# A graph layer's score table and its input rows read by SyncE and ScalarE in place of GpSimd, the first tile in five parts

## The chip, the cores and the metric

The kernel runs on one core of one Trainium2 chip. The metric is device time in microseconds for one execution. A core has TensorE (PE), VectorE (DVE), ScalarE (ACT), GpSimd (POOL) and SyncE (SP); SP, ACT and POOL can start DMAs, each on a queue of its own, and all run in the order of their own instruction streams, tied together by semaphores. PEld is TensorE's load of weights, which overlaps its matmuls.

## The reference

Two layers of a graph network on 625 nodes of 1,024 features and 10,000 edges. Each layer adds a graph part, a linear attention and a feed-forward part to x. The change lies in the first layer. Cut to what matters:

```
xn = layernorm(x)
# graph attention, 4 heads of 64
xl, xr = (down(xn) @ Wl), (down(xn) @ Wr)
e      = sum(leaky_relu(xl[src] + xr[dst]) * att)    # one score per edge and head
alpha  = softmax of e over the edges of each dst     # self loops added
gat    = segment_sum(alpha * xl[src], dst) @ W_up
# linear attention
mix    = attention(xn) @ W_o + b_o
x      = x + gat + mix
x      = x + ffn(layernorm(x))                       # quantised, 256 wide inside
...                                                  # then the second layer
```

## The kernel before, in words

Rows of x are worked in five tiles of 125 nodes (NT = 5, P = 125), tile t being nodes 125t to 125t + 124.

**Scores.** While TensorE does the linear attention's products, POOL gathers rows of xl and xr for 128 edges at a time by indirect DMA (L621), DVE and ACT make exp(score) of them, and POOL scatters these (L641) into `table`, a dense array in DRAM with four values (the heads) for each pair of source and destination. There are 79 scatters; each writes the same array, so each waits for the one before. An earlier DMA has set the table to zero, and `CT` in SBUF holds how many edges each pair has.

**Sums (weigh, sums, turn_sums, up_again).** When all scatters have landed, `load_table(t)` reads the table's tile t: 125 sources on partitions, five source groups s, 125 destinations and four heads, some 1.25 MB. `rows_dma` (L180) makes two DMAs of each read, rows 0 to 111 and rows 112 to 124. `weigh(t)` multiplies it on DVE by CT, one instruction for each s (L865), into `pT`. `sums(t)` has TensorE add up over the five s, 20 products of 65 columns (`pg`, L137; each appears as two records); DVE divides (L898 to L902); `turn_sums(t)` transposes on TensorE (L912) and copies by ACT (L916); `up_again(t)` multiplies by W_up (`px`, L928) and DVE adds that into x (L933). For tiles other than 3, `px` in PSUM already holds the attention's product with W_o.

**x and the bias.** x is read again from DRAM (`x`, 125 rows by 1,024, two DMAs a tile), since the first copy's room is used up. b_o is added by `add_bias(t)` on DVE in two additions of 512 columns (L1072); for tile 3 the kept product with the bias is added instead.

**Order.** The order on every engine is written by hand. POOL reads table tile 0, x(0), table tile 1, x(1) to x(4). DVE does weigh(0). Then a loop over p runs sums(p), turn_sums(p), weigh(p + 1), load_table(p + 2), the biases and up_again(p), with the feed-forward steps of tile p - 1 between them. add_bias(0, 1) comes in round 0 behind weigh(1), add_bias(3) in round 1 behind weigh(2), add_bias(2, 4) at the start of round 2. Round 1 also gives SP the loads of the second layer's first weights, `lin1.weights(0)` (L124: two DMAs of 1,024 KB for L1_Wk, two for L1_Wv), behind load_table(3) in the text. Round 0 makes POOL clear a margin of xnT1 and load `bq`.

The table tiles and `pT` share a pool of four buffers (`mid`), so a table tile can be read only when the buffer's last reader is done: tile 2 waits for the first sums, tile 3 for the second, tile 4 for the third.

Of the kernel before, what the change touches and what calls it, by code (L numbers as in the profile page):

```python
# [14 lines left out]
ALU = mybir.AluOpType  # L15
# [5 lines left out]
NT = 5  # L21
P = 125
# [31 lines left out]
def attempt(ctx: ExitStack, tc: tile.TileContext, w: dict, out: bass.AP, shifted: bool):  # L54

    nc = tc.nc
# [101 lines left out]
    def nodes(t):  # L158
        return slice(t * P, (t + 1) * P)
# [18 lines left out]
    def rows_dma(eng, dst, src):  # L178

        return [eng.dma_start(out=dst[lo:hi], in_=src[lo:hi]) for lo, hi in ((0, 112), (112, P))]  # L180
# [6 lines left out]
    xrows = w["x"].rearrange("(t p) d -> t p d", p=P)  # L187
# [35 lines left out]
    hold = {}  # L223

    def mid(shape, name):
        return midp.tile(shape, FP, tag="mid", name=name)

    def bigT(name):
        return big.tile([128, KC, NP], FP, tag="big", name=name, padded_shape=[128, KC, 640])
# [133 lines left out]
    with ExitStack() as st0:  # L363
# [5 lines left out]
        tview = table[0:N * N, :].rearrange("(u p d) h -> p u (d h)", u=NT, p=P)  # L369
        xnT = bigT("xnT")  # L370

        with ExitStack() as edges:
# [385 lines left out]
            def mixed(t, ks=range(KC), keep=None, then=None, paced=True, cs=(0, 1)):  # L758
                for c in cs:
                    def pe(c=c):  # L760
                        if c == 0 and ks[0] == 0:
                            hold["px", t] = ps2("px1")
                        for k in ks:
                            made = nc.tensor.matmul(hold["px", t][:P, c, :], lhsT=oT[:, k, nodes(t)], rhs=wo[c](k),  # L764
                                                    start=(k == 0), stop=(k == KC - 1 and keep is not None))
                        latest["pe"] = made.ins.name

                    def after():
                        px = hold.pop(("px", t))
                        for c in range(2):  # L770
                            nc.vector.tensor_tensor(keep[:, c, :], px[:P, c, :], bo[c][:P], op=ALU.add)

                    do(None, pe, after if keep is not None and c == 1 else None)
                    if then is not None and c == 0:
                        then()
                    if paced:
                        work(0.87 * len(ks))
# [49 lines left out]
            bo = [lin.bias(w["L0_bo"], c, tag) for c, tag in enumerate(("bk_t", "bv_t"))]  # L827
# [4 lines left out]
            kept = mid([P, 2, 512], "kept")  # L832
# [14 lines left out]
        x = xpool.tile([P, NT, D], FP, name="x")  # L847
# [3 lines left out]
        def load_table(t):  # L851

            hold["tb", t] = mid([P, NT, P, 4], "tb")
            if not shifted:
                rows_dma(nc.gpsimd, hold["tb", t].rearrange("p s d h -> p s (d h)"),
                         tview[:, :, t * 4 * P:(t + 1) * 4 * P])

        def weigh(t):

            tb, pT = hold.pop(("tb", t)), mid([P, NT, 4, P], "pT")  # L860
            hold["pT", t] = pT
            if shifted:
                exps(t, tb)
            for s in range(NT):
                nc.vector.tensor_tensor(pT[:, s], tb[:, s].rearrange("p d h -> p h d"),  # L865
                                        CT[:, s, nodes(t)].unsqueeze(1).to_broadcast([P, 4, P]), op=ALU.mult)

        def exps(t, tb):

            for h in range(4):  # L870
                sc = mix.tile([P, NP], FP, tag="qe", name="sc", bufs=1)[:, 0:N].unsqueeze(2)
                nc.sync.dma_start(out=sc, in_=table[0:N * N, :].rearrange("(t p s) h -> t p s h", t=NT, p=P)
                                  [t][:, :, h:h + 1])
                mx = late.tile([P, 1], FP, tag="mx", name="mx", bufs=1)
                nc.vector.tensor_reduce(mx, sc, AX.XY, ALU.max)
                nc.vector.tensor_scalar(mx, mx, -1.0, None, op0=ALU.mult)
                nc.scalar.activation(sc, sc, AF.Exp, bias=mx, scale=1.0)
                for s in range(NT):
                    def pe():
                        pp = ps1("pexT")  # L880
                        nc.tensor.transpose(pp[:P, :P], sc[:, nodes(s), 0], ident[:P, :P])
                        nc.vector.tensor_copy(tb[:, s, :, h], pp[:P, :P])

                    do(None, pe)
# [3 lines left out]
        def sums(t):  # L888
            pT = hold.pop(("pT", t))

            def pe():
                pg4 = hold["pg"] = ps1("pg")[:, :260].rearrange("p (h e) -> p h e", h=4)
                for h in range(4):
                    group(pg4[:P, h, :], [(pT[:, s, h, :], xl1[:, s, h, :]) for s in range(NT)])

            def after():
                pg4 = hold["pg"]
                nc.vector.tensor_scalar(dens[:, t, :], pg4[:P, :, 64], 1e-16 if shifted else 1e-30, None, op0=ALU.add)  # L898
                den = late.tile([P, 4], FP, tag="den", name="den", bufs=2)
                nc.vector.reciprocal(den, dens[:, t, :])  # L900
                go = hold["go"] = late.tile([P, 4, 64], FP, tag="go", name="go", bufs=1)
                nc.vector.tensor_tensor(go, pg4[:P, :, 0:64],  # L902
                                        den.unsqueeze(2).to_broadcast([P, 4, 64]), op=ALU.mult)

            do(None, pe, after)
# [145 lines left out]
            return p1, f1, f2, f3, f4, p5, f5  # L1051


        load_table(0)
        for t in range(NT):
            rows_dma(nc.gpsimd, x[:, t, :], xrows[t])
            if t == 0:
                load_table(1)
        weigh(0)
        kv_pieces = iter([(f, t) for t in range(NT) for f in ("key", "value")])  # L1060
        made_of = {}

        def spacer():

            f, t = next(kv_pieces)
            getattr(lin1, f)(t)

        def add_bias(*ts):
            for t in ts:
                for c in range(2):  # L1070
                    xc = x[:, t, c * 512:(c + 1) * 512]
                    nc.vector.tensor_tensor(xc, xc, kept[:, c, :] if t == 3 else bo[c][:P], op=ALU.add)  # L1072

        degree = mix.tile([128, NP], mybir.dt.int16, tag="degree", name="degree", bufs=1)

        def in_degrees():
            def pe():
                pdeg = hold["pdeg"] = ps2("pdeg")
                for h in range(2):
                    group(pdeg[:, h, :HN], [(ones[:P, :], CT[:, s, h * HN:(h + 1) * HN]) for s in range(NT)])  # L1080

            do(None, pe, lambda: nc.scalar.activation(halves(degree), hold["pdeg"][:, :, :HN], AF.Copy))

        for p in range(NT + 2):
            do()
            if p >= 2 and p != NT:
                made_of[p - 2][5]()
            if 1 <= p <= NT:
                made_of[p - 1] = ffn(p - 1)
                made_of[p - 1][0]()  # L1090
            if p == 1:
                mixed(4, cs=(0,))
            if p == 2:
                add_bias(2, 4)
                in_degrees()
            if p >= 3:
                spacer()
            if p >= 2 and p != NT:
                made_of[p - 2][6]()
            if p == 0:  # L1100
                xnT1 = bigT("xnT1")
                nc.gpsimd.memset(xnT1[:, :, N:NP], 0.0)
                lin1 = LinearAttention(xnT1, ("L1_Wq", "L1_Wk", "L1_bk", "L1_Wv", "L1_bv"), w["L1_bq"],
                                       lambda us: None, nc.gpsimd)
                lin1.large = True
            if p < NT:
                sums(p)
            if 1 <= p <= NT:
                made_of[p - 1][1]()
                do()  # L1110
                if p == NT:
                    made_of[p - 2][5]()
                made_of[p - 1][2]()
                if p == NT:
                    made_of[p - 2][6]()
            do()
            if p < NT:
                turn_sums(p)
            if p + 1 < NT:
                weigh(p + 1)  # L1120
            if p + 2 < NT:
                load_table(p + 2)
            if p < 2:
                add_bias(*((0, 1), (3,))[p])
            if p == 1:
                mixed(4, cs=(1,))
                lin1.weights(0)
                lin1.half(0, loaded=True)
            if 2 <= p <= NT:
                spacer()  # L1130
            if 1 <= p <= NT:
                made_of[p - 1][3]()
            do()
            if p < NT:
                up_again(p)
            if 1 <= p <= NT:
                made_of[p - 1][4]()
# [616 lines left out]
    for i in range(3):  # L1754
        d = 1 << i
# [240 lines left out]
```

## Time and profile before

| what | us |
|---|---|
| median of 3 runs (lowest, highest) | 2182.63 (2180.21, 2184.75) |
| the profiled execution, device time | 2200.8 |
| its span, first to last instruction | 2199.0 |
| PE busy | 2106.0 (96%) |
| DVE busy | 713.1 (32%) |
| POOL busy | 340.3 (15%) |
| ACT busy | 194.7 (9%) |
| mean granted TensorE clock | 0.984 |

How to read it: times within the kernel are microseconds from the first instruction. A timeline line has the start, the duration, the engine, the line of the source, the operation, output<-input, and how many were merged; in brackets stand the engine's idle time before it and what ended that. SPq is SP's instruction that starts a DMA. A line of the list of waits names who waited for whom, the total, how many times, and the longest. In the page's row of slices each digit is the busy share of one fortieth of the span in tenths; PEclk is TensorE's granted clock in the same way. In the stretch from 408 to 410 us the clock is 1.00, from 412 on 0.50, from 456 on 1.00. DMAs move 231 GB/s from 430 to 435 us and 340 GB/s from 465 to 470 us.

### The profile page before, as it was taken

Reading aid. Unit: us, or ns where it says so; the run is one execution under the profiler, and the core shown is the slowest. Engines: PE = TensorE matmul, PEld = TensorE weight load, DVE = VectorE, ACT = ScalarE, POOL = GpSimd, SP = SyncE. Lnnn points to the kernel's source line nnn. Section 1 sums busy time; section 2 is a strip of 40 time slices with the busy share of each in tenths; the row PEclk is TensorE's granted clock in tenths of the full one; section 3 lists DMA queues with packets and bytes.
Section 4 is the critical chain, followed back from the end, with each engine's and each line's share of the span. In section 5 each row is a group of like instructions: output and inputs, shape, how many; then the busy total and the mean of one; then the engine's idle time right before and its main releaser. Section 6 shows DMA issues by size and latency. Waiting matters only on the chain. (4 is left out here: it accounts for less than half of the span.)

```text
span 2199.0 us, 17371 instructions
## 1 busy us (share of the span) xinstructions
PE 2106.0 (96%) x6934; PEld 1205.2 (55%) x6934; DVE 713.1 (32%) x1214; ACT 194.7 (9%) x355; POOL 340.3 (15%) x349
## 2 busy tenths in 40 slices
PE   7989999489899999999999999999999999999998
PEld 6656575155445777754446777457744444444443
DVE  5776478367532740000122143222111111111012
ACT  2000110012211100000000111100000000000000
POOL 1666756500000200210000000110000000000011
PEclk9999999789999999999999999999999999999999
DMA  7623253261122110150203101022099988997742
GB/s 216 205 77 106 81 182 123 58 174 33 39 86 77 48 39 26 62 182 0 101 14 106 59 18 39 29 95 96 28 365 343 330 291 308 331 329 283 277 140 91
DMA packets 145848, 301.62 MB, mean 137 GB/s; under 512 B 12370, under 2 KB 22436, under 8 KB 145754
## 3 DMA queue, kind: packets, MB, share of 16 engines
q1 hardware_dynamic: 123700, 244.23, 31.3%
q0 software_dynamic: 17376, 46.42, 7.3%
q10 hardware_dynamic: 4678, 9.72, 1.4%
q8 instruction: 58, 0.95, 0.2%
q14 instruction: 36, 0.29, 0.0%
HBM read 277.49 MB, written 22.84 MB: 137 GB/s over the span
## 5 line engine op out<-in xcount | busy, mean ns | idle before, releaser
L137 PE MATMUL pu<-w,xgT 128*128 128x512 f32 x768 | 333.9, 593 | 1.9 <-DVE xgT L1290 1.9
L137 PEld LDWEIGHTS pu<-w,xgT 128*128 128x128 f32 x768 | 144.0, 190 | 174.8 <-issue 172.0
L137 PE MATMUL pyb<-w,hb 128*128 128x512 f32 x384 | 174.3, 598 | 2.5 <-ACT yb L105 2.1
L137 PE MATMUL pk<-w,xnT 128*125 128x512 f32 x320 | 144.7, 606 | 2.3 <-ACT xnT L1047 2.2
L137 PE MATMUL pv<-w,xnT 128*125 128x512 f32 x320 | 143.4, 599 | 1.8 <-DVE x L933 0.9
L137 PE MATMUL pq<-xnT,w 128*128 128x313 f32 x512 | 139.1, 430 | 0.9 <-DVE v L293 0.8
L137 PE MATMUL p<-tT,w 128*128 128x313 f32 x512 | 136.3, 428 | 0.4 <-DVE tT L1290 0.4
L137 PEld LDWEIGHTS pq<-xnT,w 128*128 128x128 f32 x512 | 97.7, 192 | 40.3 <-DVE v L293 1.6
L137 PEld LDWEIGHTS pyb<-w,hb 128*128 128x128 f32 x384 | 69.8, 189 | 90.9 <-issue 74.8
L1830 DVE TENSOR_TENSOR su<-pu,su 128x512 f32<-128x512 f32 x24 | 16.6, 691 | 314.6 <-ACT su L1829 314.6
L137 PEld LDWEIGHTS p<-tT,w 128*128 128x128 f32 x512 | 96.8, 190 | 37.9 <-issue 1.2
L137 PEld LDWEIGHTS pk<-w,xnT 128*125 128x125 f32 x320 | 60.8, 193 | 76.7 <-issue 74.0
L137 PEld LDWEIGHTS pv<-w,xnT 128*125 128x125 f32 x320 | 60.2, 190 | 76.5 <-issue 74.2
L641 POOL DMA_INDIRECT table<-es,at x79 | 84.0, 1063 | 56.4 <-issue 27.7
L1813 POOL DMA_INDIRECT xg<-rows_d,slots x12 | 11.4, 950 | 524.7 <-PE pxg L1820 448.9
L621 POOL DMA_INDIRECT ga<-xl_d,si x79 | 80.1, 1013 | 52.4 <-issue 20.1
L621 POOL DMA_INDIRECT gb<-xr_d,di x79 | 80.5, 1019 | 25.3 <-issue 24.7
L764 PE MATMUL px<-w,oT 128*125 128x512 f32 x160 | 69.8, 594 | 2.2 <-DVE x L933 1.6
L1179 DVE TENSOR_TENSOR z<-pz,z 125x512 fp32r<-125x512 f32 x10 | 6.9, 692 | 196.8 <-ACT z L1177 196.8
L137 PE MATMUL px<-w,hT 128*125 128x512 f32 x160 | 70.3, 592 | 0.0
L137 PE MATMUL px<-w,oT 128*125 128x512 f32 x160 | 70.3, 592 | 0.0
L137 PE MATMUL ph<-meanT,w 128*128 128x313 f32 x256 | 70.0, 426 | 0.0
(364 smaller groups left out, 2509.6 us busy)
## 6 DMA issues: line engine op xcount, KB each, us to landing
w<-in_eW_dram SPq DMA_DIRECT2D x144, 1024.0 KB
w<-in_L_Wk_dram SPq DMA_DIRECT2D x8, 1024.0 KB
w<-in_L_Wv_dram SPq DMA_DIRECT2D x8, 1024.0 KB
w<-in_L_Wq_dram SPq DMA_DIRECT2D x8, 1024.0 KB
w<-in_L_Wo_dram SPq DMA_DIRECT2D x8, 1024.0 KB
w<-in_W_self_dram SPq DMA_DIRECT2D x8, 1024.0 KB
w<-in_W_neigh_dram SPq DMA_DIRECT2D x8, 1024.0 KB
w<-in_sW_dram SPq DMA_DIRECT2D x8, 1024.0 KB
```

The costliest lines, as they stand in the source:

```text
L137: made = nc.tensor.matmul(dst, lhsT=lhsT, rhs=rhs, start=(i == 0), stop=(i == len(pairs) - 1))
L621: got = nc.gpsimd.indirect_dma_start(out=ab[g][side][0:p, j, :], out_offset=None, in_=src[:, :], in_offset=bass.IndirectOffsetOnAxis(ap=ix ...
L641: nc.gpsimd.indirect_dma_start(out=table[:, :], out_offset=bass.IndirectOffsetOnAxis(ap=at[0:p, lo + j:lo + j + 1], axis=0), in_=es[0:p, l ...
L764: made = nc.tensor.matmul(hold["px", t][:P, c, :], lhsT=oT[:, k, nodes(t)], rhs=wo[c](k), start=(k == 0), stop=(k == KC - 1 and keep is no ...
L1179: nc.vector.tensor_tensor(low, src, high.bitcast(FP), op=ALU.subtract)
L1813: nc.gpsimd.indirect_dma_start(out=xg, out_offset=None, in_=rows_d[:, :], in_offset=bass.IndirectOffsetOnAxis(ap=slots[:, b:b + 1], axis=0))
L1830: nc.vector.tensor_tensor(su, pu[:, 0, :], su, op=ALU.mult)
```

## The change

Three edits.

1. `load_table(0)` reads the five source groups apart, s = 0, 2, 4 by SP and s = 1, 3 by ACT, each again in rows 0 to 111 and 112 to 124: ten DMAs where there were two. Each of the five instructions of weigh(0) waits for its own part.
2. The other table tiles and x are read by SP, in place of POOL. Table tile 1 is now read behind x(1), where it was behind x(0).
3. add_bias(0, 1) is called right behind weigh(0), ahead of the loop, in place of behind weigh(1) in round 0. On DVE the four additions now stand before the division of the first sums.

In SP's stream the reads of table tiles 2 and 3 now precede the loads of L1_Wk and L1_Wv, and tile 4 follows them. The order of PE's instructions is unchanged.

```diff
         def load_table(t):
 
             hold["tb", t] = mid([P, NT, P, 4], "tb")
-            if not shifted:
-                rows_dma(nc.gpsimd, hold["tb", t].rearrange("p s d h -> p s (d h)"),
+            if not shifted and t == 0:
+                for s in range(NT):
+                    rows_dma((nc.sync, nc.scalar)[s % 2], hold["tb", t][:, s].rearrange("p d h -> p (d h)"),
+                             tview[:, s, t * 4 * P:(t + 1) * 4 * P])
+            elif not shifted:
+                rows_dma(nc.sync, hold["tb", t].rearrange("p s d h -> p s (d h)"),
                          tview[:, :, t * 4 * P:(t + 1) * 4 * P])
...
         load_table(0)
         for t in range(NT):
-            rows_dma(nc.gpsimd, x[:, t, :], xrows[t])
-            if t == 0:
+            rows_dma(nc.sync, x[:, t, :], xrows[t])
+            if t == 1:
                 load_table(1)
         weigh(0)
+        add_bias(0, 1)
...
-            if p < 2:
-                add_bias(*((0, 1), (3,))[p])
+            if p == 1:
+                add_bias(3)
```

`add_bias` itself moves up in the text, unchanged. `shifted` is the second attempt, which runs only if the first found numbers out of range; in the runs here it doesn't.

More of the change, by code (lines that the diff above doesn't have):

```diff
@@ L1051, in ffn, with add_bias @@
             return p1, f1, f2, f3, f4, p5, f5
+        def add_bias(*ts):
+            for t in ts:
+                for c in range(2):
+                    xc = x[:, t, c * 512:(c + 1) * 512]
+                    nc.vector.tensor_tensor(xc, xc, kept[:, c, :] if t == 3 else bo[c][:P], op=ALU.add)
         load_table(0)
         for t in range(NT):
-            rows_dma(nc.gpsimd, x[:, t, :], xrows[t])
-            if t == 0:
+            rows_dma(nc.sync, x[:, t, :], xrows[t])
+            if t == 1:
                 load_table(1)
         weigh(0)
+        add_bias(0, 1)
         kv_pieces = iter([(f, t) for t in range(NT) for f in ("key", "value")])
@@ L1066, in spacer @@
             getattr(lin1, f)(t)
[L1068 to L1072, printed above, removed]
         degree = mix.tile([128, NP], mybir.dt.int16, tag="degree", name="degree", bufs=1)
```

## The prediction

> **What bounds the kernel now.** I read the page's busy times and slices first, then the list of waits, then the timelines of PE, DVE, POOL and SP between 404 and 486 us.
>
> ```profile
> PE 2106.0 (96%) x6934; PEld 1205.2 (55%) x6934; DVE 713.1 (32%) x1214; ACT 194.7 (9%) x355; POOL 340.3 (15%) x349
> ...
> PE   7989999489899999999999999999999999999998
> ...
> PEclk9999999789999999999999999999999999999999
> ```
>
> TensorE is busy for 96% of the span. One slice, the eighth (385 to 440 us), shows 4, and the clock is low there. The list of waits names it:
>
> ```profile
> PE pg L137 <- DVE pT L865: 32.5, 5, 31.4
> ```
>
> One wait of 31.4 us, ended by VectorE's first weighing. On PE:
>
> ```profile
> 404.80 2.31 PE L764 MATMUL px<-w,oT 128*125 128x512 f32 x5
> 438.51 0.68 PE L137 MATMUL pg<-xl,pT 125*125 125x65 f32 x2 [31.40 <-DVE pT L865]
> ...
> 442.30 6.98 PE L137 MATMUL pg<-xl,pT 125*125 125x65 f32 x32 [0.26 <-DVE pT L865]
> 450.21 0.68 PE L912 MATMUL pgoT<-ident,go 125*128 125x125 f32 x2 [0.93 <-DVE go L902]
> 451.42 5.52 PE L928 MATMUL px<-wu,goT 128*125 128x512 f32 x8 [0.53 <-ACT goT L916]
> 458.54 7.13 PE L764 MATMUL px<-w,oT 128*125 128x512 f32 x16 [1.59 <-DVE x L933]
> ```
>
> On DVE, the weighing waited for the table; then came its wait for the sums, the second weighing, the four bias additions and L933, which frees PE:
>
> ```profile
> 437.42 4.83 DVE L865 TENSOR_TENSOR pT<-tb,CT 125x500 f32<-125x500 f32 x5 [16.36 <-DMA tb<-table]
> 449.32 0.16 DVE L898 TENSOR_SCALAR dens<-pg 125x4 f32<-125x4 f32 x1 [7.07 <-PE pg L137]
> ...
> 450.07 4.87 DVE L865 TENSOR_TENSOR pT<-tb,CT 125x500 f32<-125x500 f32 x5
> 454.84 0.70 DVE L1072 TENSOR_TENSOR x<-x,bk_t 125x512 f32<-125x512 f32 x1
> ...
> 457.25 1.24 DVE L933 TENSOR_TENSOR x<-px,x 125x1024 f32<-125x1024 f32 x1
> ```
>
> On POOL, the last scatters, then the first table tile, x(0), the second tile and x(1) on one queue:
>
> ```profile
> 426.50 0.85 POOL L641 DMA_INDIRECT table<-es,at  x1 [1.91 <-issue]
> 429.02 1.55 POOL L180 DMA_DIRECT2D tb<-table  x2 [1.67 <-issue]
> 430.55 1.11 POOL L180 DMA_DIRECT2D x<-in_x_dram  x2
> 431.64 1.46 POOL L180 DMA_DIRECT2D tb<-table  x2
> 433.10 1.08 POOL L180 DMA_DIRECT2D x<-in_x_dram  x2
> ```
>
> and on SyncE's queue two weight loads that the change puts reads ahead of:
>
> ```profile
> 462.26 3.81 SPq L124 DMA_DIRECT2D w<-in_L_Wk_dram  x2
> 477.15 3.80 SPq L124 DMA_DIRECT2D w<-in_L_Wv_dram  x2
> ```
>
> The chain here is: last scatter lands (428.40 by the trace's completion events of its semaphore), table tile lands (436.57 for the 112 rows, 437.39 for the 13), weighing, sums, L933. From 458.54 on PE is nearly always busy until the end, so what this chain gains goes through to the end.
>
> [...] POOL's issue at 429.02 has its first packet at 430.63 (1.6 us), SP's at 462.26 has it at 463.31 (1.05 us). [...] an issue on SP takes 0.3 to 0.45 us in this trace. [...]
>
> **Step 1, the first table tile.** Before, 428.40 to 437.42 is 9.0 us: 0.6 until POOL starts, 1.6 until the first packet, the rest for packets and completion with x(0) behind. After, ten DMAs are issued by SP (parts 0, 2, 4) and ScalarE (1, 3). Both only wait for the last scatter; ScalarE has nothing to do from 413.35 to 450.99. SP starts 0.02 us after its event (xin: landing 6.18, issue 6.20). The price of a hardware DMA I take from the first Wk load, 1,024 KB: first packet after 1.05 us, 32 packets of 2,048 bytes per DMA engine at 84 ns (2.7 us), last completion event 1.26 us later (467.33), in sum 5.07. A part is 125 rows of 2,000 bytes, 8 packets per engine, 0.66 us; with the other engine's part beside it 1.3. So parts 0 and 1 land 1.05 + 1.3 + 1.26 = 3.6 us after the scatter, at 432.05. That is an estimate; the trace has no such small table read on this path. Ends: a part alone, completed 0.8 us after its packets (the earliest event of the Wk load), 2.5 us, 430.9; all four parts together, packets as slow as POOL's table packets (median 341 ns for 6,000 bytes, so 114 per row): 1.05 + 32 x 0.114 + 1.26 = 6.0, 434.4. Gain at the first weighing: 437.42 - 432.05 = **5.4 us** (3.0 to 6.5).
>
> **Step 2, the other parts.** Weighings start 0.97 us apart, as before. The built program has eight semaphores for these DMAs, so part 4 isn't issued before parts 0 and 1 have landed. Issued at 432.05 to 432.4, it lands at 1.05 + 0.66 + 1.26 = 3.0 us later, 435.4. It is due at 432.05 + 4 x 0.97 = 435.9. No loss; the fifth weighing ends at 436.9 instead of 442.25. At the slow end it lands at 438.0 and the fifth ends at 439.1, a gain of 3.1.
>
> **Step 3, x(0) and x(1) on SP and the biases.** x(0) and x(1), 1 MB, are issued from 432.7 to 434.2 behind part 4: 16 packets of 4,096 bytes per engine at 159 ns (measured at 340 to 352 us) are 2.5 us; they land by about 437.5. The four additions, 0.6 us each, end by about 439.5. They now stand before dens on DVE, but dens can't start before PE's sums end: 442.30 to 449.28 are 6.98 us at half clock, so 443.9 after. Margin 4 us. Without that cover each us that x(1) is late costs one.
>
> **Step 4, the second tile.** It is issued behind x(1) at 434.1, lands by about 440.7 (40 packets per engine, 3.4 us, after x(1)'s) and is due when go ends, 444.8. Moreover pT(1) no longer has four additions between it and L933.
>
> **Step 5, L933.** Before, DVE was ready at 457.25 and PE's px ended at 456.94; after, px ends at 456.94 - 5.4 = 451.5 and DVE, without the 2.4 us of additions, ends pT(1) near 449.7. The gain is PE's 5.4, plus 0.3 at most, which I leave out: the 5.52 us of px were cut by a clock rise 3.7 us into it. [...]
>
> **Step 6, what SP holds back.** Wk (before at 462.26) now stands behind tiles 2 and 3; tile 3 waits for the sums of tile 1 (POOL issued it at 470.29). Wk is then issued about 3 us later than before, in place of 5.4 us earlier, and with tile 3 ahead lands near 477; the first pk runs at 502.96 less 5.4. Cost 0; bare of this cover, 8 us. Wv waits for PE at 477.15 as before. Tile 4 passes from POOL to SP behind Wv and waits for the third sums (499.7); the next load on SP is at 570.38. POOL loses its 20 issues of 0.5 to 0.9 us, off the path.
>
> **Sum.** 5.4 + 0 + 0 + 0 + 0 - 0. Against the profiled execution, 2200.8 us (span 2199.0, 1.8 around it): 2195.4. The median of the runs is 2182.63, 18.2 below the profiled one; the same 5.4 gives **2177.2 us**. About 0.2% (4.4 us) is what a measurement of this kernel can tell from no change.
>
> **Rivals.**
> - The parts land together and late. For it: POOL's table packets took 341 ns per 6,000 bytes, far slower than SP's 84 per 2,048, and it may be the table, not the path, that is slow. Against: they ran with x(0) and tile 1 in the air. Step 1 and 2's slow end with another 0.5: gain 2.5, 2180.1 us.
> - Tile 1 becomes late: on SP it stands behind x(1). At POOL's rate (2.99 MB from the first packet at 430.63 to 445.66, 200 GB/s) its 3.5 MB take until 448.3; L933 allows 452.2 - 4.9 = 447.3. Loss 1.0: gain 4.4, 2178.2 us. Against: SP's weight loads ran at 340 GB/s from 465 to 470 us.
> - Slower: x(1) holds DVE's queue. Dens, go and PE's transposes stand behind the biases. It costs from a landing at about 442.7 on, and eats the whole gain at 448. If x(1) lands at 451, as late behind its issue as POOL's third x (issue 436.86, landing 449.63, 12.8 us), plus 4 for semaphore rounds, the loss is 3: 2185.6 us. Against: there some 2 MB stood ahead of it, here less than 1 MB.
>
> That the reads aren't moved is no rival: the built order of instructions shows them on SP and ScalarE, and five separate waits for the five weighings.
>
> **How the numbers follow.** Forecast 0.64, late parts 0.22, late tile 1 0.10, slower 0.04. The range takes in the fast end[...], 6.5 + 1.4 = 7.9 (2174.7), and the late parts less 0.9 for the scatter (2181.0). Faster by over 0.2%: 0.92 of the forecast and half of the late tile, 0.64; slower 0.04; the rest 0.32.
>
> **What would show it.** First weighing near 432 and PE's first pg near 433; five weighings without gaps (a wait for part 4 says step 2 is off); additions ended before PE's 32 sums (else step 3); pT(1) with no DMA wait (else step 4); no wait for w at the first pk (else step 6). A first weighing after 434.5 makes the forecast wrong.

## The result and the profile after

| | before | after |
|---|---|---|
| median of the runs (8 each) | 2179.89 | 2175.41 |
| lowest to highest | 2177.78 to 2184.75 | 2173.95 to 2176.47 |
| ratio, with its 95% interval | 1 | 0.9978 (0.9969 to 0.9988) |
| profiled execution's span | 2199.04 | 2174.57 |

The change saves 4.5 us; 5.4 were forecast, and 2175.41 lies in the range of 2174.7 to 2181.0. The two spans are not to be subtracted: the profiled execution of the kernel before was some 20 us longer in its first 400 us, which no edit touches. So every time of a stage below counts **from the landing of the last scatter**, the last completion event of its semaphore (428.40 us in the kernel before, 407.91 after). From there to the end it is 1770.63 us before and 1766.65 after: 4.0 less.

The page of the changed kernel, its busy times and two rows of the slices:

```profile
PE 2096.6 (96%) x6934; PEld 1201.3 (55%) x6934; DVE 712.8 (33%) x1214; ACT 194.8 (9%) x355; POOL 326.9 (15%) x329
...
PE   8999999499999999999999999999999999999998
...
PEclk9999999699999999999999999999999999999999
```

PE's busy time can't be read as a gain or a loss here, since it depends on the clock: 32 records of the first sums took 6.98 us at a granted clock of 0.50, the 40 of the second sums 4.48 us at 1.00. The eighth slice still shows 4. The list of waits has the same entry, shorter:

```profile
PE pg L137 <- DVE pT L869: 29.2, 5, 28.1
```

The 31.4 us became 28.1; L869 is the L865 of before, four lines further down, and L937 is L933. The difference of 3.3 us isn't the gain, since TensorE began this wait 21.3 us ahead of the scatter's landing in the kernel before and 22.6 ahead of it here. PE's timeline:

```profile
413.39 0.68 PE L137 MATMUL pg<-xl,pT 125*125 125x65 f32 x2 [28.09 <-DVE pT L869]
...
417.19 6.98 PE L137 MATMUL pg<-xl,pT 125*125 125x65 f32 x32 [0.26 <-DVE pT L869]
425.10 0.68 PE L916 MATMUL pgoT<-ident,go 125*128 125x125 f32 x2 [0.92 <-DVE go L906]
426.31 5.76 PE L932 MATMUL px<-wu,goT 128*125 128x512 f32 x8 [0.53 <-ACT goT L920]
433.38 7.13 PE L764 MATMUL px<-w,oT 128*125 128x512 f32 x16 [1.31 <-DVE x L937]
```

and DVE's:

```profile
412.30 4.83 DVE L869 TENSOR_TENSOR pT<-tb,CT 125x500 f32<-125x500 f32 x5 [11.71 <-DMA tb<-table]
418.32 0.69 DVE L1062 TENSOR_TENSOR x<-x,bk_t 125x512 f32<-125x512 f32 x1 [1.19 <-DMA x<-in_x_dram]
...
424.21 0.16 DVE L902 TENSOR_SCALAR dens<-pg 125x4 f32<-125x4 f32 x1 [2.44 <-PE pg L137]
...
426.46 4.88 DVE L869 TENSOR_TENSOR pT<-tb,CT 125x500 f32<-125x500 f32 x5 [1.42 <-DMA tb<-table]
432.10 1.22 DVE L937 TENSOR_TENSOR x<-px,x 125x1024 f32<-125x1024 f32 x1 [0.76 <-PE px L932]
```

The weighings and sums have kept their durations and only lie earlier. Two DMA waits are new: the additions wait for x (1.19, and 0.86 for x(1)), then the second weighing waits 1.42 us for table tile 1. Neither shows in the result: L937 waited for PE's px, 0.76 us longer than DVE needed.

On SP, the reads follow each other; the first line merges parts 0, 2 and 4, and part 4 was held back as foreseen (issued at 4.07 us, where part 2 was issued at 0.87):

```profile
407.97 4.77 SPq L180 DMA_DIRECT2D tb<-table  x6
413.14 1.93 SPq L180 DMA_DIRECT2D x<-in_x_dram  x4
415.11 0.87 SPq L180 DMA_DIRECT2D tb<-table  x2
```

SP started 0.05 us after the landing, where the prediction had 0.02. Parts 0 and 1 landed at 4.30 and 4.52 us, part 4 at 6.85, x(0) and x(1) at 10.29 and 12.54, tile 1 at 18.46 (17.26 before).

This table puts the stage side by side, with the experiments that follow ("weighed" is the end of the fifth weighing, "divided" the start of DVE's division, when PE's sums are done; "rest" is from L933/L937 to the end):

| kernel | first weighing | weighed | tile 1 landed | divided | second weighing | px end | L933/L937 | rest | ratio of runs |
|---|---|---|---|---|---|---|---|---|---|
| before | 9.01 | 13.85 | 17.26 | 20.92 | 21.67 to 26.54 | 28.54 | 28.84 | 1741.8 | 1 |
| after | 4.39 | 9.22 | 18.46 | 16.30 | 18.55 to 23.43 | 24.15 | 24.19 | 1742.5 | 0.9978 |
| c_after | 4.49 | 9.32 | 18.40 | 16.40 | 18.50 to 23.37 | 24.24 | 24.27 | 1742.2 | 0.9972 |
| c2_after | 4.19 | 9.02 | 17.24 | 16.09 | 17.33 to 22.19 | 24.94 | 24.97 | 1745.1 | 0.9974 |
| e1_bias_back | 4.23 | 9.08 | 17.35 | 16.15 | 17.45 to 22.30 | 24.66 | 24.70 | 1742.2 | 0.9989 |
| e2_one_read | 7.68 | 12.52 | 16.88 | 19.59 | 20.34 to 25.18 | 27.66 | 27.69 | 1742.4 | 0.9993 |
| e3_sp_alone | 3.11 | 8.42 | 19.88 | 15.49 | 19.97 to 24.84 | 23.18 | 24.76 | 1744.0 | 0.9981 |
| e4_parts_on_pool | 3.68 | 9.66 | 19.55 | 16.73 | 19.65 to 24.54 | 24.01 | 26.82 | 1745.8 | 0.9988 |
| e6_tile1_first | 4.59 | 9.42 | 13.58 | 19.93 | 20.67 to 25.53 | 28.20 | 28.24 | 1742.3 | 0.9993 |
| e7_order | 3.11 | 8.45 | 16.51 | 15.53 | 16.53 to 21.39 | 24.38 | 24.42 | 1745.3 | 0.9959 |
| e8_sums_by_part | 3.15 | 8.68 | 15.89 | 12.95 | 15.91 to 20.78 | 20.95 | 20.99 | 1742.3 | 0.9970 |
| e8_again | 2.91 | 8.62 | 17.78 | 12.71 | 17.80 to 22.67 | 21.05 | 22.60 | 1746.7 | 0.9959 |
| e9_x_behind | 7.78 | 12.61 | 21.28 | 19.68 | 21.37 to 26.24 | 28.10 | 28.14 | 1741.9 | 0.9992 |
| e10_sums_alone | 4.55 | 9.40 | 19.03 | 14.73 | 19.12 to 23.99 | 23.27 | 23.88 | 1745.8 | 0.9976 |

The runs came in three sets, each with the kernel before beside it: e1, e2, e3 and e6 (kernel before 2180.44 us), then c_after, e7, e8_sums_by_part and e9 (2207.02), then c2_after, e4, e8_again and e10 (2179.24). Medians are compared within a set only. The ratios' intervals are 0.0006 to 0.0020 to each side, so 1.3 to 4.4 us: what the stage shows to 0.1 us, the runs can confirm only roughly. To set the lines of the experiments beside the table: the last scatter landed at 406.37 us in e3, 406.83 in e4, 408.02 in e6, 405.83 in e8_again and 432.73 in e9.

### The profile page after: what moved, and what is told of

It reads as the page before. It is cut to its first block, busy times and chain, and to the rows that moved or that the text cites. A ratio compares the mean times of both kernels' runs of the same rounds, so it can differ in the third digit from the quotient of the medians.

```text
span 2174.6 us, 17390 instructions
## 1 busy us (share of the span) xinstructions
PE 2096.6 (96%) x6934; PEld 1201.3 (55%) x6934; DVE 712.8 (33%) x1214; ACT 194.8 (9%) x355; POOL 326.9 (15%) x329
```

## The experiments

In the expectations, theory 1 is the account that I held at that point (small parts that land early, and other DMAs that share the DMA engines with them); theory 2 is the rival account in that run. The question of the first ones is what gains: the reading in parts, the queue, or the bias. The later ones ask what holds L937 back once the parts are early.

**c_after and c2_after: the changed kernel again,** as a control.

> The changed kernel again, on the chip of the runs beside it. Times are counted from the landing of the last scatter. As in its first profile: first weighing at 4.4 us, L937 at 24.2, ratio to the kernel before 0.998. It shows how far these numbers repeat, before others are held against them.

> The changed kernel once more, on the chip of the runs beside it, for their comparison: L937 at 24.2 us after the last scatter, ratio 0.998.

The medians were 2201.13 against 2207.02 (ratio 0.9956 to 0.9988) and 2174.46 against 2179.24 (0.9967 to 0.9982). Up to the second weighing the stage repeats within some 0.3 us, but for tile 1, which landed between 17.2 and 18.5. px took 5.76, 5.74 and 6.75 us in the three profiles: the clock rose 22.6, 22.6 and 24.4 us after the landing. The spread is 1.0 us; the 1.4 at the fast end of the prediction's range was an estimate of it. Against the one profile of the kernel before, L937 gains 4.65, 4.57 and 3.87 us.

**e2_one_read: the queue alone.** Tile 0 in one read (two DMAs) on SP.

```diff
-            if not shifted and t == 0:
-                for s in range(NT):
-                    rows_dma((nc.sync, nc.scalar)[s % 2], hold["tb", t][:, s].rearrange("p d h -> p (d h)"),
-                             tview[:, s, t * 4 * P:(t + 1) * 4 * P])
-            elif not shifted:
+            if not shifted:
                 rows_dma(nc.sync, hold["tb", t].rearrange("p s d h -> p s (d h)"),
```

> The changed kernel with the first table tile read whole, by SP alone, two DMAs, as the other tiles. Theory 1 (the parts let the first weighing start before the rest has landed): the first weighing comes 1.05 + 40 x 0.082 + 1.26 = 5.6 us after the last scatter's landing in place of 4.4, and the run is 1.2 us longer. Theory 2 (the queue alone is the gain: no wait for POOL, and nothing queued in front): 4.4 us as in after, no difference. If the table's rows come slowly when the whole tile is one DMA, it is 6.5 or more.

The first weighing came at 7.68, the ratio is 0.9993 (0.9985 to 1.0001). The whole tile lands at 7.59, slower than either theory's number; it is the third outcome that the expectation names, rows that come slowly when the tile is one read. The first weighing gains 1.3 us on the kernel before; the rest of after's 4.6 is missing, and the runs show no gain that is clear of noise.

**e9_x_behind: is the whole tile slow by itself?** As e2, with x and tile 1 issued only behind the first weighing.

```diff
...
+        weigh(0)
         for t in range(NT):
-            rows_dma(nc.sync, x[:, t, :], xrows[t])
+            got = rows_dma(nc.sync, x[:, t, :], xrows[t])
+            if t == 0:
+                behind(got[0], latest["weighed"])
...
-        weigh(0)
```

> As e2_one_read (the first tile in one read on SyncE), but x(0), x(1) and the second tile are issued only behind the first weighing. It tells why e2_one_read's tile took 7.6 us. If the traffic behind it slows it: first weighing at about 5.6 us. If a read of 1.25 MB takes that long by itself: at 7.0 or later. x and the second tile come later than in e2_one_read, so L937 says nothing here.

SP's issues in this run, then DVE's first weighing:

```profile
432.79 0.87 SPq L180 DMA_DIRECT2D tb<-table  x2
441.63 1.60 SPq L180 DMA_DIRECT2D x<-in_x_dram  x4
```

```profile
440.52 4.83 DVE L865 TENSOR_TENSOR pT<-tb,CT 125x500 f32<-125x500 f32 x5 [15.12 <-DMA tb<-table]
```

Nothing of x or tile 1 was in the air until 441.63, and the tile still took until 7.69 us after the scatter (440.42 in this run). So the 1.25 MB take that long by themselves, and the traffic behind them is not the cause. In the trace the packets run from 1.04 us to 7.03 us, 209 GB/s; their median is 114 ns for 2,000 bytes where those of e3's parts took 82. POOL's packets in the kernel before, 341 ns for 6,000 bytes, come to the same 114: read whole, the table is as slow on one queue as on the other.

**e4_parts_on_pool: the parts alone.** The kernel before with tile 0 in five parts on GpSimd's queue; x, tile 1 and the biases stay where they were.

```diff
+            if not shifted and t == 0:
+                for s in range(NT):
+                    rows_dma(nc.gpsimd, hold["tb", t][:, s].rearrange("p d h -> p (d h)"),
+                             tview[:, s, t * 4 * P:(t + 1) * 4 * P])
-            if not shifted:
+            elif not shifted:
```

> The kernel before with one edit: the first tile is read in the five parts, all on GpSimd's queue. If reading in parts is what gains, and the queue only adds its own delays (0.6 us until it starts, 1.6 to the first packet, some 0.75 us an issue): first weighing at about 5 us, the others paced by the issues at 1.5 us each, so that the fifth ends at about 12 instead of 13.9, and L933 1.5 to 2 us earlier than before. If it is the queue that gains: first weighing at 7 us or later and the fifth at 14, no gain.

```profile
410.50 1.04 DVE L869 TENSOR_TENSOR pT<-tb,CT 125x500 f32<-125x500 f32 x1 [11.01 <-DMA tb<-table]
```

It was better than expected at its head: part 0 landed at 3.65 and the first weighing ran at 3.68, 5.3 us earlier than before and even 0.7 earlier than in the changed kernel. The issues took 0.54 us, not 0.75, and the fifth weighing ended at 9.66. The ratio is 0.9988 (0.9981 to 0.9995). Of the 4.2 us at the weighings' end only 2.0 reach L937. DVE's timeline tells why:

```profile
426.47 4.89 DVE L869 TENSOR_TENSOR pT<-tb,CT 125x500 f32<-125x500 f32 x5 [2.08 <-DMA tb<-table]
431.25 0.72 DVE L1076 TENSOR_TENSOR x<-x,bk_t 125x512 f32<-125x512 f32 x1
...
433.65 1.25 DVE L937 TENSOR_TENSOR x<-px,x 125x1024 f32<-125x1024 f32 x1
```

PE's px ended at 24.01 us (430.84), but DVE was still at the second weighing, late by its wait of 2.08 us for tile 1, and then had the four additions ahead of L937. This is what edit 3 of the change is there to prevent. With the queue and the biases of the change as well (c2_after, same set), L937 came at 24.97 and the median was 2174.46 against e4's 2177.49, 3.0 us less; the two ratios' intervals still touch.

**e1_bias_back: the change without edit 3.**

```diff
-        add_bias(0, 1)
...
-            if p == 1:
-                add_bias(3)
+            if p < 2:
+                add_bias(*((0, 1), (3,))[p])
```

> The changed kernel with its third edit undone: the additions to x(0) and x(1) stand behind the second weighing again. In the profile of after, the second weighing ended at 431.34 us and TensorE's px at 432.07, so 0.73 us are free there. Theory 1 (the additions matter now, since the second tile lands late and DVE is nearly as late as PE): 2.4 us of additions less 0.73 make L937 (the addition of px) 1.6 us later after the last scatter's landing, 25.8 us in place of 24.2, and the run about 1.6 us longer. Theory 2 (the prediction's step 5: moving them is worth 0.3 us at most): 24.2 to 24.5, no difference.

L937 at 24.70, between the two: tile 1 landed at 17.35 here, so DVE's second weighing and the additions ended at 24.65, together with px at 24.66. The price of edit 3's absence is thus an estimate of max(0, tile 1's landing + 7.3 - px's end), where 7.3 us are the second weighing and the four additions: about 0 here and 2.8 in e4, where the additions also stand behind the second weighing (L937 came 2.8 behind px). With after's own tile 1 (18.46) and px (24.15) it would be 1.6; that is worked out, not run. The median was 2178.06 (ratio 0.9983 to 0.9995), some 2 us more than after's ratio gives, as theory 1 had it, but the two intervals overlap, and this profile shows 0.5 us at L937. What edit 3 alone is worth in the runs stays open.

**e3_sp_alone: all five parts on SP.**

```diff
-                    rows_dma((nc.sync, nc.scalar)[s % 2], hold["tb", t][:, s].rearrange("p d h -> p (d h)"),
+                    rows_dma(nc.sync, hold["tb", t][:, s].rearrange("p d h -> p (d h)"),
```

> The changed kernel with all five parts read by SP, none by ScalarE. In after the first part took 4.4 us in place of the 3.6 forecast. Theory 1 (ScalarE's parts share the DMA engines with the first part, whose packets come between them, and SP's second part follows): with SP alone the parts come one after the other, the first weighing 0.4 + 1.05 + 0.66 + 1.1 = 3.2 us after the landing, the others 0.74 us apart by SP's issues, under DVE's 0.97; the run is about 1.2 us shorter. Theory 2 (a table read takes 4.4 us here whatever else is in the air): 4.3 to 4.5 us, and the run is the same; if the issues on one queue are what limits, later parts leave gaps between the weighings and it is longer.

```profile
409.48 3.14 DVE L869 TENSOR_TENSOR pT<-tb,CT 125x500 f32<-125x500 f32 x3 [10.44 <-DMA tb<-table]
```

Theory 1 was right at the head: part 0 landed at 3.02 and the weighing ran at 3.11, 1.3 us earlier than with ScalarE's help. The other parts landed one after the other (4.18, 4.93, 6.33, 6.83), and the five weighings end at 8.42. px ended 1.0 earlier than after, at 23.18, but tile 1 landed at 19.88 and L937 came at 24.76, so the shortening of 1.2 us that theory 1 forecast for the run didn't come. Ratio 0.9981 (0.9973 to 0.9989).

**e6_tile1_first: tile 1 ahead of x.**

```diff
         load_table(0)
+        load_table(1)
         for t in range(NT):
             rows_dma(nc.sync, x[:, t, :], xrows[t])
-            if t == 1:
-                load_table(1)
```

> The changed kernel with the second table tile read ahead of x(0) and x(1). In after it landed 18.5 us after the last scatter, 1.4 us after DVE was ready for it; x(1) landed at 12.5. Theory 1 (what stands in DVE's queue behind a late x(1) is late by as much: the prediction's slower rival): the second weighing no longer waits, but x(1) lands at about 18.5, its additions end at 19.8, and the division of the first sums, due at 16.3, waits for that: 3.5 us later, L937 at 27.7 in place of 24.2, the run 3 to 3.5 us longer. Theory 2 (the late second tile is what costs in after, and the additions have room): L937 at 23.4 or earlier, the run shorter by 0.7.

This makes the slower rival's mechanism happen:

```profile
423.61 0.69 DVE L1062 TENSOR_TENSOR x<-x,bk_t 125x512 f32<-125x512 f32 x1 [6.17 <-DMA x<-in_x_dram]
...
426.74 0.69 DVE L1062 TENSOR_TENSOR x<-x,bk_t 125x512 f32<-125x512 f32 x1 [1.84 <-DMA x<-in_x_dram]
427.35 0.68 DVE L1062 TENSOR_TENSOR x<-x,bv_t 125x512 f32<-125x512 f32 x1
427.96 0.15 DVE L902 TENSOR_SCALAR dens<-pg 125x4 f32<-125x4 f32 x1
```

Tile 1 landed at 13.58, but x(1) only at 18.63. The division stands behind its additions and starts at 19.93 with no idle time before it, 3.5 us after PE's sums. L937 comes at 28.24, and all but 0.6 us of the gain is gone (ratio 0.9985 to 1.0001).

**e7_order: order alone.** Parts on SP as in e3, then x(0), tile 1, x(1); add_bias(1) in round 1.

```diff
...
-            if t == 1:
+            if t == 0:
                 load_table(1)
         weigh(0)
-        add_bias(0, 1)
+        add_bias(0)
...
+                add_bias(1)
```

> The changed kernel, with the five parts on SyncE alone, then x(0), the second tile and x(1) in this order, the biases of x(0) behind the first weighing and those of x(1) a round later. Theory 1 (what holds L937 once the parts are early is the second tile, and before it x(1) on VectorE's queue; each is cured by order alone): weighing at 3.1 us, sums at about 15.5, second tile landed by 16, second weighing from 16.3, L937 at 23.2 to 23.5, about 0.8 us earlier than in the changed kernel. Theory 2 (the second tile is late wherever it stands, because the bytes of the first 3.5 MB set it): it lands at 17 or later and L937 stays at 24 or later.

Tile 1 landed at 16.51 and the second weighing ran from 16.53 to 21.39, as theory 1 said; yet L937 came at 24.42, later than theory 1's 23.2 to 23.5. Now px alone was last: it began 0.8 us earlier than after, at 17.62, and took 6.76 us, as the clock rose only at 23.8. With after's 5.76 it would have ended at 23.4, an estimate. So order cures the tile, and the clock took the gain back in this profile. The median was 2198.77, 2.4 less than the changed kernel's beside it, with an interval (0.9940 to 0.9979) that overlaps with that one's.

**e8_sums_by_part and e8_again: sums that follow the weighings.** As e7, with the loops of the sums turned; this applies to all five tiles.

```diff
-                for h in range(4):
-                    group(pg4[:P, h, :], [(pT[:, s, h, :], xl1[:, s, h, :]) for s in range(NT)])
+                for s in range(NT):
+                    for h in range(4):
+                        made = nc.tensor.matmul(pg4[:P, h, :], lhsT=pT[:, s, h, :], rhs=xl1[:, s, h, :],
+                                                start=(s == 0 and h == 0), stop=(s == NT - 1 and h == 3))
...
```

> As e7_order, and PE's 20 products of the first sums run with the part outside and the head inside, so that they can follow the weighings; the same applies to all later sums. Theory 1 (after the parts are early, PE's sums that wait for all five weighings, 7 us at half clock, are what keeps L937 back): sums end at about 10.5 to 13 us instead of 15.5, px 2.5 to 5 earlier, and L937 moves with it as far as the second weighing lets it: 20.4 to 23. If instead the second tile is what comes last, L937 stays where e7_order has it.

> The kernel of e8_sums_by_part again, since its first timing had an interval too wide to set it against the changed kernel. If what its stage showed goes through to the end: L937 at 21.0 us after the last scatter and 3.2 us less than the changed kernel in the runs, ratio 0.9965 to the kernel before. If the later order of sums or of biases costs elsewhere what the stage gains: 0.998 or more.

PE and DVE in the second of them:

```profile
409.84 8.66 PE L899 MATMUL pg<-xl,pT 125*125 125x65 f32 x40 [25.18 <-DVE pT L869]
```

```profile
418.54 0.16 DVE L905 TENSOR_SCALAR dens<-pg 125x4 f32<-125x4 f32 x1 [1.47 <-PE pg L899]
...
423.63 4.87 DVE L869 TENSOR_TENSOR pT<-tb,CT 125x500 f32<-125x500 f32 x5 [4.26 <-DMA tb<-table]
```

The 40 records now run without a gap from the first weighing on, where in the changed kernel 32 of them waited for the fifth. The division starts at 12.7 to 13.0, 3.3 to 3.6 us earlier than after. L937 came at 20.99 in the first profile and, with tile 1 at 17.78 in place of 15.89, at 22.60 in the second: 3.2 and 1.6 us earlier than after (3.3 and 2.4 earlier than c_after and c2_after, each in its own set). The medians are 2198.61 (changed kernel beside it 2201.13) and 2171.65 (2174.46): 2.5 and 2.8 us less, with ratios to before of 0.9957 to 0.9983 and 0.9947 to 0.9971. Those overlap with the changed kernel's in both cases. Five of e8_again's six runs took 2172.22 us or less, and one of c2_after's sixteen did. So that this version beats the changed kernel is likely, and shown for the stage alone.

**e10_sums_alone: the turned sums in the changed kernel.** The edit is the diff just shown and nothing else.

> The changed kernel with the sums' product loop turned (part outside, head inside) and nothing else. If the second tile, which lands at 17.4 to 18.5 us here, is what comes next: sums end near 13 us, px earlier, but L937 only at 23.4, 0.8 us earlier than in the changed kernel. If the sums alone held L937: at 21.5 or earlier.

L937 at 23.88, a gain of 0.3 to 1.1 on the three profiles of the changed kernel; px ended at 23.27 but the second weighing had waited 3.56 us for tile 1 (19.03), and L937 came directly behind it. Median 2175.88 (0.9966 to 0.9986), no gain that could be measured. The sums ended at 14.3, not 13, since they start with the first weighing and take 8.66 us without a gap. So the turned loop pays only where tile 1 is early too.

## Why the prediction was right, point by point

**Sum.** 5.4 forecast; 4.5 in the runs (2.6 to 6.8 by the ratio's interval), 4.65 at L937 in the first profile. Right in mechanism; one term was too large. The absolute time owes something to luck: 2177.2 and its range rest on 2182.63, a median of three runs, and the eight runs beside the changed kernel gave 2179.89. A gain of exactly 5.4 from there would have been 2174.5, just below the range.

**Step 1, the term that was mis-sized.** Part 0 was put at 3.6 us after the scatter and landed at 4.30; the gain is 9.01 - 4.39 = 4.6, not 5.4. The term is what the other engine's parts cost part 0: it was put at 0.64 us (1.3 of packets in place of 0.66), and e3, with nothing of ACT's in the air, shows 4.30 - 3.02 = 1.28. In after, SP's first 125 packets were through at 2.88 us, when ACT had sent more than 112; in e3 they were at 2.14. That is 0.74 us, near what was forecast. The other 0.54 is the completion, 1.42 us behind those packets in after and 0.88 in e3; four parts were in the air by then, not the two that were reckoned with, but what delays it wasn't isolated. That a part alone came out right, 3.02 where the step's terms give 2.97, is luck: its packets took 1.15 us and not 0.66, its completion 0.88 and not 1.26. The step also never said which of its two ingredients gains. e2 and e4 do: on SP's queue alone 1.3 us, in parts alone 5.3.

**Step 2, right.** The five weighings ran without gaps (4.39 to 9.22) and part 4, issued at 4.07, landed at 6.85 for a use at 8.19.

**Step 3, right in its outcome, by a smaller margin.** x(1) landed at 12.54, forecast 9.1; the additions ended near 13.9, and DVE still waited 2.44 us for PE where 4 were forecast. e6 shows what lies behind the margin.

**Step 4, wrong without a cost.** Tile 1 was to land by 12.3 and landed at 18.46, behind the time at which DVE was free for it (17.13). Reads were priced at the weight loads' rate; in fact the 3.5 MB came between 1 and 18.46 us, 200 GB/s, the very rate of POOL's queue that I gave to the rival. Both figures leave out what was read behind the second tile. With it, 4.07 MB had moved by 18.46 us in after, 233 GB/s, and 3.42 MB from 2.22 to 17.26 us on POOL's queue in the kernel before, 227 GB/s. So these reads ran at much the same rate on both queues, while the weight loads ran at 340 on SP's; what in the reads sets it wasn't isolated. From 16 to 18 us, 89 packets of x(2) moved and only 16 of tile 1, so x(2), which nothing needs yet, may be part of tile 1's delay; no run held it back. The rival's threshold, 447.3 or 18.9 us on this scale, was missed by half a microsecond; e3 (19.88) and e10 (19.03) crossed it, and there L937 came behind DVE.

**Step 5, right but for one clause.** L933 gained 4.65: 4.39 from px, 0.26 since DVE is ready. "0.3 at most" for the moved additions holds only against an early tile 1; in e4 the second weighing and the additions end 2.8 us behind px. px took 5.52 us before and 5.76 after; over all profiles it ran from 5.18 (e4) to 6.76 (e7). That this pair lay within 0.3 us of each other is chance.

**Step 6, right.** SP issued the load of the second layer's first weight, Wk, at 445.74, 4.0 us later behind the scatter than before (3 were forecast); it had landed by 459.58, and the first product that uses it, pk, ran at 477.81 with no wait.

**Rivals.** Late parts: didn't come. Its suspicion that the table itself is slow was right for a whole tile (114 ns for 2,000 bytes on both queues, e9); what it missed is that the first part needn't wait for the rest (e4). Late tile 1: its mechanism came, its loss did not. Its sum had two slips: it counted the 17.6 us of bytes from POOL's first packet at 430.63, where SP's at 429.47 gives 447.1, or 18.7 us; and its limit of 452.2 for L933 isn't the 451.5 of step 5. In after DVE had 0.76 us to spare. Slower: only with the order of e6. Its 4 us for semaphore rounds were an estimate that no run tested.

## What to carry to other kernels

When a consumer works through a large read piece by piece, ask when the first piece lands. Here, reading in pieces on one queue in the order of use brought the first weighing forward by 5.3 us on POOL's queue (before to e4) and by 4.6 on SP's (e2 to e3). The faster queue was worth 1.3 us with the tile read whole and 0.6 in pieces, and a second queue for the same pieces put the first one back by 1.3. Then ask at once what comes late next, and price it at the rate of like reads (here 200 GB/s) and not at that of the best loads in the trace (here 340). Two cures that each moved L937 by 0.3 us or less in their profiles against the first one of the changed kernel (tile 1's order with all parts on SP, the turned sums) moved it by 1.6 to 3.2 together.

## What the runs showed of the hardware

- **A half-clock stretch that comes and goes.** "rest" in the table is 1741.8 to 1742.5 us in eight profiles and 1744.0 to 1746.7 in the other six, with the same instructions or nearly so. In those six, the clock falls to 0.5 once more or twice, beginning between 23 and 60 us after the scatter, for 3.41 us in all (rest 1744.0), 6.8 (1745.1 to 1745.8) or 10.2 (1746.7). The same 20 matmuls in c2_after and then in the profile of after (mean granted clock from 445 to 520 us: 0.95 and 1.00):

```profile
462.07 8.55 PE L137 MATMUL pdeg<-CT,ones 125*128 125x313 f32 x20 [1.50 <-DVE x L1035]
```

```profile
462.89 5.54 PE L137 MATMUL pdeg<-CT,ones 125*128 125x313 f32 x20 [1.50 <-DVE x L1035]
```

  Both stand behind the same two short idle times, 1.3 and 1.5 us with 1.0 us of matmuls between. What makes the clock fall in the one and not in the other was not isolated. This stretch is why I read gains off the stage and not off the span.
- **The clock came back during px.** In the kernel before, the clock was 0.50 from 410.75 to 455.13 us and rose 3.7 us into px; in after it was 0.50 from 389.53 to 430.49 and rose 4.2 us into px; in c2_after and e7 it rose 6.2 us into it. In all four, 6.98 or 6.99 us of sums without a gap had ended ahead of px with the clock still at 0.50. How far into px the rise comes decides how long px takes: 5.52, 5.76, 6.75 and 6.76 us. What sets the moment of the rise was not shown.
- **The first part landed early on both queues.** The first 250 KB landed 3.0 us behind the scatter on SP (e3) and 3.65 on POOL (e4), with the other parts issued behind them; the tile read whole took 7.6 (e2) to 9.0 (before), though all five parts on one queue are in by 6.8 (e3) to 8.3.
